# A four-layer graph network on one core: x moved to DRAM during the passes of layers 2 and 3, 12 more row buffers in its place, and their loop issued in program order

## The chip, the core and the metric

The kernel runs on one core of a Trainium2 chip. The metric is device time in microseconds of one execution; the time given is the median of the runs shown. [...]

The engines are called as in the profile: PE is TensorE's matrix multiply and PEld its weight load, DVE is VectorE, ACT is ScalarE, POOL is GpSimd, and SP is SyncE, which here only issues transfers.

## What is computed

6250 nodes with 128 features each pass through four graph layers over the same 200000 edges (src, dst, sorted by dst). Every layer normalises x over its features, applies relu, computes something per edge, sums it per node and adds the result to x. Cut to its core:

```python
h = jnp.maximum(_layernorm(x), 0.0)
x = x + mlp0(h + segment_sum(h[src], dst))                       # layer 0
h = jnp.maximum(_layernorm(x), 0.0)
x = x + mlp1(segment_sum((h @ W_in)[src'] * filter(edge_attr), ...))   # layer 1

h = jnp.maximum(_layernorm(x), 0.0)                              # layer 2
xl, xr = h @ Wl + bl, h @ Wr + br
m = leaky_relu(xl[src] + xr[dst] + edge_weight1 @ We, 0.2)
logits = m @ att
alpha = softmax of logits over the edges of one dst
out = segment_sum(xl[src] * alpha[:, None], dst) + bias_out
x = x + batchnorm(gelu(h + out))

h = jnp.maximum(_layernorm(x), 0.0)                              # layer 3
score = sum(h[dst] * tanh(h[src] + rel[edge_type]), axis=-1)
attn = exp(score - max) / segment_sum(exp(score - max), src)[src]
x = x + leaky_relu((h + segment_sum(attn[:, None] * h[dst], src)) @ W.T, 0.2)
```

## The kernel before

x, the node features, lies in SBUF for the whole kernel as one tile of 128 partitions x 49 x 128 floats (25 KB a partition). Nodes are numbered so that partition p holds nodes 49p to 49p+48.

Each layer first writes the table that its edges read to DRAM (h_tab, y_tab, l_tab and r_tab, g_tab), then runs a pass over the edges. In layers 0, 2 and 3 the pass gathers rows by index; layer 1 computes messages, scatters them to DRAM in the order of src, and reads them back. Layer 3 sums over src and walks the edges in that order, whose indices layer 1 leaves in o_tab and e_tab. The edges are cut into NG = 391 groups of FE = 512 edges, FT = 4 columns of 128 edges each. A group's sums fall on a window of at most 64 neighbouring nodes, so that they are a matrix product with a one-hot matrix, added to an accumulator acc in SBUF at an offset that is loaded as a register. Where the edges aren't sorted as needed, general2 and general3 run in place of windows2 and windows3; with these inputs the window path runs.

Layers 2 and 3 need a softmax over edges. Their passes (sums2, sums3) share the driver in_chunks, which works in chunks of CG = 12 groups and pipelines by steps. In step g it issues, in this order:

- fetch(g): four indirect gathers of 128 rows each into the group's row tile m, issued by POOL (a helper at L298), the load of the window's rows win by SP, every second group the load of a row of indices, and the one-hot matrix hotT on DVE;
- weighted(a) for the oldest group whose softmax weights are known: the one-hot hot on DVE, and in layer 2 the rows scaled by their weights into v on ACT (L1209);
- sums for the group weighted in the step before: PE products ps;
- near(g-1): the PE product pz of hotT and win, four matmuls of two passes each (L1119, L1414), in layer 3 followed by tanh on ACT;
- scores(g-2): on DVE, from pz and m (L1125 to L1128, L1422);
- add: the products of the step before are added into acc on DVE;
- one stage of weights for the chunk whose scores are complete: a generator of six stages in layer 2 (L1136 to L1194), three in layer 3 (L1431 to L1451), one stage a step.

A row tile m is thus in use from its gather until ACT has scaled it (layer 2), or until PE has read it as the stationary operand of ps (L1473, layer 3). The tiles come from a pool mp with 2 x CG + 1 = 25 buffers of 2 KB a partition in layer 2, and 2 x CG + 3 = 27 in layer 3. The other buffers: 4 windows win, 3 pairs of hotT, 3 banks of pz, 2 of ps, 3 of v.

The order in which instructions stand in each engine's queue is chosen by the framework's scheduler, which simulates the program and takes instructions by readiness and priority; the text above gives the priority. Semaphores between engines are placed by the framework too.

After the pass, finish2 and finish3 send the sums of the weights through the small DRAM table d_tab into node order, scale acc, and add the layer's result to x in blocks of CJ = 7 columns. All loads and stores that are not gathers go through the queues of SP and ACT.

Of the kernel before, what the change touches and what calls it, by code (L numbers as in the profile page):

```python
# [9 lines left out]
F32 = mybir.dt.float32  # L10
# [10 lines left out]
D = 128  # L21
# [47 lines left out]
def gnn_kernel(ctx: ExitStack, tc: tile.TileContext, t, out):  # L69
# [74 lines left out]
    def nodes(table):  # L144

        return table[0:NP, :].rearrange("(p j) f -> p j f", j=J)
# [11 lines left out]
    o_tab = dram.tile([IDS - 1, P, NG * FT], I32, name="o_tab")  # L158
    e_tab = dram.tile([2, EP], F32, name="e_tab")
    d_tab = dram.tile([2, NP], F32, name="d_tab")  # L160
    sums = [[dram.tile([ROWS, D], F32, name=f"sum{i}_{k}") for k in range(K)] for i in range(2)]
    softs = [[dram.tile([ROWS, W2], F32, name=f"soft{i}_{k}") for k in range(K)] for i in range(2)]

# [829 lines left out]
    with tc.tile_pool(name="h", bufs=1) as hp, tc.tile_pool(name="y", bufs=2) as yp, \  # L993
            tc.tile_pool(name="y_ps", bufs=2, space=PSUM) as pp:
        h = hp.tile([P, J, D], F32, name="h")
        norm_relu(h)
        nc.scalar.dma_start(nodes(k_tab), h)
        rest = hp.tile([FW, D], F32, name="rest")
        nc.vector.memset(rest, 0.0)
        nc.scalar.dma_start(r_tab[NP:, :], rest)  # L1000
        for c, js in quads:
            if js[0] == c:
                y = yp.tile([P, CJ, D], F32, name="y")
                r = yp.tile([P, CJ, D], F32, name="r")
            u = turned(yp, pp, js, h)
            py = pp.tile([P, 4, 2 * D], F32, name="py")
            for i, j in enumerate(js):
                nc.tensor.matmul(py[:, i, :], ones[0:1, :], b_lr, start=True, stop=False)
                nc.tensor.matmul(py[:, i, :], u[:, i * P:(i + 1) * P], w_lr, start=False, stop=True)
            cs = slice(js[0] - c, js[-1] + 1 - c)  # L1010
            nc.scalar.copy(y[:, cs, :], py[:, :len(js), :D])
            nc.vector.tensor_copy(r[:, cs, :], py[:, :len(js), D:])
            if js[-1] == c + CJ - 1:
                nc.sync.dma_start(nodes(l_tab)[:, c:c + CJ, :], y)
                nc.sync.dma_start(nodes(r_tab)[:, c:c + CJ, :], r)

    def in_chunks(sp, fetch, near, scores, weights, weighted, sums, add):

        sc, ms, todo = None, [], []
        one, two, held = None, None, None
        hot, part = None, None
        g = 0
        while g < NG or one or two or held or todo or hot or part:
            new = (g, fetch(g)) if g < NG else None
            new_hot = None
            if todo:
                a, m, i, ex, scale, more = todo.pop(0)  # L1030
                new_hot = a, weighted(a, m, ex[:, i * FT:(i + 1) * FT], *more), scale
            new_part = (hot[0], sums(hot[0], hot[1]), hot[2]) if hot else None
            new_two = (one[0], near(*one)) if one else None
            if two:
                b, got = two
                i = b % CG
                if i == 0:
                    sc, ms = sp.tile([P, CG * FT], F32, name="sc"), []
                ms.append((b, scores(b, got, sc[:, i * FT:(i + 1) * FT])))
            if part:  # L1040
                add(*part)
            if held:
                try:
                    next(held[0])
                except StopIteration as e:
                    ex, scale, *more = e.value
                    todo += [(a, m, a % CG, ex, scale if i == 0 else None, more)
                             for i, (a, m) in enumerate(held[1])]
                    held = None
            if two and (b % CG == CG - 1 or b == NG - 1):  # L1050
                held = weights(b // CG * CG, len(ms) * FT, sc), ms
                next(held[0])
            one, two, hot, part = new, new_two, new_hot, new_part
            g += 1

    def windows2():

# [7 lines left out]

    def sums2(st, acc):
        lp = st.enter_context(tc.tile_pool(name="ld", bufs=1))
        mp = st.enter_context(tc.tile_pool(name="em", bufs=2 * CG + 1))
        wp = st.enter_context(tc.tile_pool(name="ew", bufs=3))
        rp = st.enter_context(tc.tile_pool(name="er", bufs=2))  # L1070
        sp = st.enter_context(tc.tile_pool(name="es", bufs=2))
# [25 lines left out]
        row = {}  # L1097

        def fetch(g):
            m = mp.tile([P, FT, D], F32, name="m")  # L1100
            for j in range(FT):
                gather(m[:, j, :], l_tab, src[:, g * FT + j:g * FT + j + 1])
            nc.sync.dma_start(win[g % 4][:FW, :], r_tab[bass.ds(starts(g, SP), FW), :])
            h = hots[g // RW % 3]
            if g % RW == 0:
                n = min(RW, NG - g) * FE
                row["d"] = rp.tile([FW, RW * FE], I32, name="row")
                nc.sync.dma_start(row["d"][:, :n], t["dst_row"][:, g * FE:g * FE + n].partition_broadcast(FW))
# [121 lines left out]
    def finish2(acc):  # L1230

        with tc.tile_pool(name="f1", bufs=1) as f1, tc.tile_pool(name="fin", bufs=2) as fp, \
                tc.tile_pool(name="fin_ps", bufs=2, space=PSUM) as pp:
            den = f1.tile([P, J], F32, name="den")
            nc.sync.dma_start(d_tab[0:1, :], acc[0:1, 1, :NP])
            nc.sync.dma_start(den, d_tab[0].rearrange("(p j) -> p j", j=J))
# [388 lines left out]
```

## Time and profile before

| what | us |
|---|---|
| median of 3 runs (9888.56 to 9907.39) | 9891.45 |
| profiled execution, its own time | 11254.5 |
| profiled execution, span from first to last instruction | 11252.7 |
| layer 0, from its first gather to its last | 77.6 to 2432.2 |
| layer 1's read-back products, first to last | 5150.1 to 5828.4 |
| layer 2, gathers, first to last | 6068.1 to 8578.8 |
| layer 2, last product of the sums | 8661.7 |
| layer 3, gathers, first to last | 8789.9 to 11107.3 |
| layer 3, last product of the sums | 11178.5 |

Busy shares of the whole span: PE 74%, PEld 56%, DVE 48%, ACT 18%, POOL 56%.

How to read the views that follow. A line of groups gives source line, engine, operation, tiles and count, then busy us and mean ns of one, then the idle us of the engine just before these instructions and what ended that idle time. "Issue" there means that the profile shows nothing that the engine was waiting for. A line of windows gives a stretch of the span, its length, busy us and count for each engine, the mean granted clock of TensorE (1 is full speed), the busy share of the 16 DMA engines and the GB/s they moved. A line of the timeline gives start, duration, engine, line and operation, with idle time before it in brackets. Some lines can stand for a helper: L298 is the gather of every layer.

### The profile page before, as it was taken

What the parts mean: (1) busy time and instruction counts of PE and PEld (TensorE: products, weight loads), DVE (VectorE), ACT (ScalarE), POOL (GpSimd) and SP (SyncE); (2) the same over time, 40 slices, a digit from 0 to 9 for tenths busy, and PEclk for the clock granted to TensorE, in tenths of its full rate; (3) what the DMA queues carried; (4) which work ended last, traced back from release to release, by engine and by line L of the source; (5) the groups of instructions that cost most, each with busy time, mean ns of one, the idle gap of its engine ahead of it and who ended that gap; (6) DMA issues with size and microseconds to landing.
All of it is one profiled execution on the core that took longest, in us unless ns stands there. A gap on an engine that the chain in (4) does not pass through costs nothing.

```text
span 11252.7 us, 122557 instructions
## 1 busy us (share of the span) xinstructions
PE 8329.9 (74%) x34445; PEld 6310.5 (56%) x34445; DVE 5379.8 (48%) x21948; ACT 1987.7 (18%) x4844; POOL 6250.5 (56%) x6269
## 2 busy tenths in 40 slices
PE   3788888757999988888995666666666267766776
PEld 2444444445666656558982555555555266666665
DVE  4455555413333434334442555555555355555556
ACT  0000000004333434331111122112122111111111
POOL 5666666644666666661003566666663466666663
PEclk9955555555555555555555666666666555555556
DMA  2111111113333333335542222222222233333333
GB/s 66 45 45 44 44 44 44 45 42 92 92 94 93 95 94 94 95 92 139 158 113 67 66 68 69 67 69 68 67 69 60 81 95 95 96 95 94 96 94 88
DMA packets 457374, 893.54 MB, mean 79 GB/s; under 512 B 149642, under 2 KB 231743, under 8 KB 455763
## 3 DMA queue, kind: packets, MB, share of 16 engines
q1 hardware_dynamic: 245552, 456.89, 14.6%
q0 software_dynamic: 200192, 412.80, 13.8%
q10 hardware_dynamic: 10918, 15.65, 0.5%
q8 instruction: 290, 4.75, 0.2%
q14 instruction: 422, 3.46, 0.1%
HBM read 753.95 MB, written 130.80 MB: 79 GB/s over the span
## 4 chain that ended last, share of the span: by engine, by line
PE 55%; issue 13%; DVE 12%; another core or an unknown queue 12%; POOL 3%; DMA 1%; ACT 1%; DVEq 0%; SPq 0%; ACTq 0%; POOLq 0%
PE pw L905 6%; PE ps L959 6%; PE pf L896 6%; PE py L899 6%; PE ps L825 4%; PE ps L1216 4%; PE pz L1119 3%; PE pz L1414 3%; PE ps L1473 3%; POOL m L298 3%; PE pq L778 3%; PE pq L779 2%; PE sizes L746 2%; PE ps L1218 2%
## 5 line engine op out<-in xcount | busy, mean ns | idle before, releaser
L302 POOL DMA_INDIRECT m_tab<-m,pos x1564 | 1569.6, 1004 | 1141.4 <-issue 539.6
L298 POOL DMA_INDIRECT m<-l_tab,src x1564 | 1614.2, 1032 | 1047.9 <-issue 564.7
L298 POOL DMA_INDIRECT m<-g_tab,dst x1564 | 1527.0, 976 | 851.9 <-issue 400.6
L298 POOL DMA_INDIRECT m<-h_tab,src x1564 | 1537.2, 983 | 830.3 <-issue 420.3
L1414 PE MATMUL pz<-win,hotT 128*128 128x128 f32 x3128 | 797.7, 414 | 406.7 <-issue 322.2
L1473 PE MATMUL ps<-hot,m 128*128 128x64 f32 x3128 | 724.0, 402 | 367.5 <-issue 164.3
L825 PEld LDWEIGHTS ps<-hot,m 128*128 128x128 f32 x3128 | 739.3, 327 | 384.8 <-issue 160.0
L899 PEld LDWEIGHTS py<-win,hotT 64*128 64x128 f32 x3128 | 667.8, 313 | 490.5 <-issue 414.7
L1414 PEld LDWEIGHTS pz<-win,hotT 128*128 128x128 f32 x3128 | 678.9, 307 | 449.7 <-issue 436.5
L825 PE MATMUL ps<-hot,m 128*128 128x64 f32 x3128 | 736.8, 411 | 260.5 <-DVE hot L822 101.3
L1473 PEld LDWEIGHTS ps<-hot,m 128*128 128x128 f32 x3128 | 677.9, 315 | 441.3 <-issue 186.8
L1119 PE MATMUL pz<-win,hotT 128*128 128x128 f32 x3128 | 690.8, 373 | 302.3 <-issue 247.6
L905 PEld LDWEIGHTS pw<-L_gnn_W_f,sp_r 128*128 128x128 f32 x3128 | 682.4, 321 | 382.3 <-issue 327.0
L905 PE MATMUL pw<-L_gnn_W_f,sp_r 128*128 128x128 f32 x3128 | 798.5, 434 | 126.7 <-DVE sp_r L931 92.7
L899 PE MATMUL py<-win,hotT 64*128 64x128 f32 x3128 | 775.9, 424 | 135.0 <-issue 107.2
L909 DVE TENSOR_TENSOR m<-pw,L_gnn_b_f_b 128x512 f32<-128x512 f32 x391 | 269.8, 690 | 1226.4 <-PE pw L905 431.6
L1216 PE MATMUL ps<-hot,v 128*128 128x64 f32 x3128 | 604.7, 342 | 273.7 <-issue 198.0
L1209 ACT ACTIVATE v<-m,ex 128x128 f32<-128x128 f32 x1564 | 489.2, 389 | 1762.4 <-remote 873.2
L1119 PEld LDWEIGHTS pz<-win,hotT 128*128 128x128 f32 x3128 | 571.6, 265 | 396.5 <-issue 337.3
L896 PE MATMUL pf<-row_a,L_gnn_W_f 20*128 20x512 f32 x782 | 758.8, 1077 | 23.3 <-DMA row<-in_dst_row 15.3
L1216 PEld LDWEIGHTS ps<-hot,v 128*128 128x128 f32 x3128 | 567.0, 262 | 306.9 <-issue 281.2
L959 PE MATMUL ps<-hot,m 128*128 128x64 f32 x3128 | 671.0, 420 | 18.7 <-DMA m<-m_tab 18.5
(318 smaller groups left out, 12281.2 us busy)
## 6 DMA issues: line engine op xcount, KB each, us to landing
m<-m_tab SPq DMA_DIRECT2D x391, 262.0 KB
row<-in_dst_row SPq DMA_DIRECT2D x390, 256.0 KB
row<-e_tab SPq DMA_DIRECT2D x390, 256.0 KB
row_w<-in_w_row SPq DMA_DIRECT2D x195, 256.0 KB
m<-h_tab,src POOLq DMA_INDIRECT x1564
m_tab<-m,pos POOLq DMA_INDIRECT x1564
m<-l_tab,src POOLq DMA_INDIRECT x1564
m<-g_tab,dst POOLq DMA_INDIRECT x1564
```

The costliest lines, as they stand in the source:

```text
L298: nc.gpsimd.indirect_dma_start(out=dst, out_offset=None, in_=table[:], in_offset=bass.IndirectOffsetOnAxis(ap=idx, axis=0))
L302: nc.gpsimd.indirect_dma_start(out=table[:], out_offset=bass.IndirectOffsetOnAxis(ap=idx, axis=0), in_=src, in_offset=None, **kw)
L825: nc.tensor.matmul(ps, m[:, j, :], hot[:, j, :], start=(j == 0), stop=(j == FT - 1))
L896: nc.tensor.matmul(pf, w_f1, row["a"][:, es], start=True, stop=True)
L899: nc.tensor.matmul(py[:, j, :], hot[:, j * P:(j + 1) * P], w, start=True, stop=True)
L905: nc.tensor.matmul(pw[:, j, :], sp[:, j * P:(j + 1) * P], w_f2, start=True, stop=True)
L959: nc.tensor.matmul(ps, m[:, j, :D], hot[:, j, :], start=(j == 0), stop=(j == FT - 1))
L1119: nc.tensor.matmul(pz[:, j, :], hot[:, j * P:(j + 1) * P], win[g % 4], start=True, stop=True)
L1209: nc.scalar.activation(v[:, j, :], m[:, j, :], AF.Copy, scale=ex[:, j:j + 1])
L1216: nc.tensor.matmul(ps[:, 0, :], v[:, j, :], hot[:, j, :], start=(j == 0), stop=(j == FT - 1))
L1414: nc.tensor.matmul(pz[:, j, :], hot[:, j * P:(j + 1) * P], win[g % 4], start=True, stop=True)
L1473: nc.tensor.matmul(ps[:, 0, :], m[:, j, :], hot[:, j, :], start=(j == 0), stop=(j == FT - 1))
```

## The change

It has five parts.

- A DRAM table x_tab is added. After the normalisation that opens layer 2, x is stored to it through SP's queue; in layer 3 through ACT's queue.
- The pool mp is replaced by a ring of fixed tiles: 25 (27) of its own, followed by 12 that are slices of x, columns 4k to 4k+3 each. Group g uses entry g modulo 37 (39). The last of the 49 columns of x isn't used.
- x_back loads x again from x_tab in seven blocks through SP's queue: in finish2 ahead of everything else, in finish3 after the loads of den.
- The loop of in_chunks is put under manual_schedule for PE, DVE, ACT and POOL: their instructions in the loop keep the order of the text. SP isn't among them.
- The four gathers of a group are issued from the last column to the first.

The general path is not changed. The diff; the loop's body is only indented, which is left out here:

```diff
--- before.py
+++ after.py
@@ -158,6 +158,7 @@
     o_tab = dram.tile([IDS - 1, P, NG * FT], I32, name="o_tab")
     e_tab = dram.tile([2, EP], F32, name="e_tab")
     d_tab = dram.tile([2, NP], F32, name="d_tab")
+    x_tab = dram.tile([NP, D], F32, name="x_tab")
     sums = [[dram.tile([ROWS, D], F32, name=f"sum{i}_{k}") for k in range(K)] for i in range(2)]
     softs = [[dram.tile([ROWS, W2], F32, name=f"soft{i}_{k}") for k in range(K)] for i in range(2)]
 
@@ -995,6 +996,7 @@
         h = hp.tile([P, J, D], F32, name="h")
         norm_relu(h)
         nc.scalar.dma_start(nodes(k_tab), h)
+        nc.sync.dma_start(nodes(x_tab), x)
         rest = hp.tile([FW, D], F32, name="rest")
         nc.vector.memset(rest, 0.0)
         nc.scalar.dma_start(r_tab[NP:, :], rest)
@@ -1014,6 +1016,15 @@
                 nc.sync.dma_start(nodes(l_tab)[:, c:c + CJ, :], y)
                 nc.sync.dma_start(nodes(r_tab)[:, c:c + CJ, :], r)
 
+    def rows_ring(pool, n):
+
+        return [pool.tile([P, FT, D], F32, name=f"m{k}") for k in range(n)] + [
+            x[:, k * FT:(k + 1) * FT, :] for k in range(J // FT)]
+
+    def x_back():
+        for c in range(0, J, CJ):
+            nc.sync.dma_start(x[:, c:c + CJ, :], nodes(x_tab)[:, c:c + CJ, :])
+
     def in_chunks(sp, fetch, near, scores, weights, weighted, sums, add):
 
 
@@ -1023,35 +1034,37 @@
         one, two, held = None, None, None
         hot, part = None, None
         g = 0
-        while g < NG or one or two or held or todo or hot or part:
...
+        order = {mybir.EngineType.PE, DVE, mybir.EngineType.Activation, mybir.EngineType.Pool}
+        with tc.manual_schedule(engines=order):
+            while g < NG or one or two or held or todo or hot or part:
...
 
     def windows2():
 
@@ -1065,7 +1078,7 @@
 
     def sums2(st, acc):
         lp = st.enter_context(tc.tile_pool(name="ld", bufs=1))
-        mp = st.enter_context(tc.tile_pool(name="em", bufs=2 * CG + 1))
+        ring = rows_ring(lp, 2 * CG + 1)
         wp = st.enter_context(tc.tile_pool(name="ew", bufs=3))
         rp = st.enter_context(tc.tile_pool(name="er", bufs=2))
         sp = st.enter_context(tc.tile_pool(name="es", bufs=2))
@@ -1097,8 +1110,8 @@
         row = {}
 
         def fetch(g):
-            m = mp.tile([P, FT, D], F32, name="m")
-            for j in range(FT):
+            m = ring[g % len(ring)]
+            for j in reversed(range(FT)):
                 gather(m[:, j, :], l_tab, src[:, g * FT + j:g * FT + j + 1])
             nc.sync.dma_start(win[g % 4][:FW, :], r_tab[bass.ds(starts(g, SP), FW), :])
             h = hots[g // RW % 3]
@@ -1231,6 +1244,7 @@
 
         with tc.tile_pool(name="f1", bufs=1) as f1, tc.tile_pool(name="fin", bufs=2) as fp, \
                 tc.tile_pool(name="fin_ps", bufs=2, space=PSUM) as pp:
+            x_back()
             den = f1.tile([P, J], F32, name="den")
             nc.sync.dma_start(d_tab[0:1, :], acc[0:1, 1, :NP])
             nc.sync.dma_start(den, d_tab[0].rearrange("(p j) -> p j", j=J))
@@ -1338,6 +1352,7 @@
         h = hp.tile([P, J, D], F32, name="h")
         norm_relu(h)
         nc.sync.dma_start(nodes(g_tab), h)
+        nc.scalar.dma_start(nodes(x_tab), x)
         rest = hp.tile([FW, D], F32, name="rest")
         nc.vector.memset(rest, 0.0)
         nc.scalar.dma_start(g_tab[NP:, :], rest)
@@ -1359,7 +1374,7 @@
 
     def sums3(st, acc, top):
         lp = st.enter_context(tc.tile_pool(name="ld", bufs=1))
-        mp = st.enter_context(tc.tile_pool(name="em", bufs=2 * CG + 3))
+        ring = rows_ring(lp, 2 * CG + 3)
         wp = st.enter_context(tc.tile_pool(name="ew", bufs=3))
         rp = st.enter_context(tc.tile_pool(name="er", bufs=3))
         sp = st.enter_context(tc.tile_pool(name="es", bufs=2))
@@ -1391,8 +1406,8 @@
         row = {}
 
         def fetch(g):
-            m = mp.tile([P, FT, D], F32, name="m")
-            for j in range(FT):
+            m = ring[g % len(ring)]
+            for j in reversed(range(FT)):
                 gather(m[:, j, :], g_tab, dst[:, g * FT + j:g * FT + j + 1])
             nc.sync.dma_start(win[g % 4][:R, :], g_tab[bass.ds(starts(g, SP, first_b), FW), :])
             if g % RW == 0:
@@ -1492,6 +1507,7 @@
             for k in range(2):
                 nc.sync.dma_start(d_tab[k:k + 1, :], acc[k * R:k * R + 1, 1, :NP])
                 nc.sync.dma_start(den[:, k, :], d_tab[k].rearrange("(p j) -> p j", j=J))
+            x_back()
             pt = pp.tile([P, 1], F32, name="pu")
             nc.tensor.matmul(pt, ones[0:1, :], top[:, 0:1], start=True, stop=True)
             last_ = f1.tile([P, 1], F32, name="last_")
```

More of the change, by code (lines that the diff above doesn't have):

```diff
@@ L1025, in in_chunks @@
         g = 0
-        while g < NG or one or two or held or todo or hot or part:
[L1027 to L1043, printed above, removed]
-                    next(held[0])
[L1045 to L1054, printed above, removed]
@@ new lines, in in_chunks @@
+        order = {mybir.EngineType.PE, DVE, mybir.EngineType.Activation, mybir.EngineType.Pool}
+        with tc.manual_schedule(engines=order):
+            while g < NG or one or two or held or todo or hot or part:
+                new = (g, fetch(g)) if g < NG else None
+                new_hot = None
+                if todo:
+                    a, m, i, ex, scale, more = todo.pop(0)
+                    new_hot = a, weighted(a, m, ex[:, i * FT:(i + 1) * FT], *more), scale
+                new_part = (hot[0], sums(hot[0], hot[1]), hot[2]) if hot else None
+                new_two = (one[0], near(*one)) if one else None
+                if two:
+                    b, got = two
+                    i = b % CG
+                    if i == 0:
+                        sc, ms = sp.tile([P, CG * FT], F32, name="sc"), []
+                    ms.append((b, scores(b, got, sc[:, i * FT:(i + 1) * FT])))
+                if part:
+                    add(*part)
+                if held:
+                    try:
+                        next(held[0])
+                    except StopIteration as e:
+                        ex, scale, *more = e.value
+                        todo += [(a, m, a % CG, ex, scale if i == 0 else None, more)
+                                 for i, (a, m) in enumerate(held[1])]
+                        held = None
+                if two and (b % CG == CG - 1 or b == NG - 1):
+                    held = weights(b // CG * CG, len(ms) * FT, sc), ms
+                    next(held[0])
+                one, two, hot, part = new, new_two, new_hot, new_part
+                g += 1
```

## The prediction

> **What bounds the kernel now.** I read four views in this order: busy time by engine, the same for the two loops alone, the groups of the gathers with their idle time, and what the engines waited for. A stretch of the timeline then decides between two readings.
>
> The two loops that the change touches run from 6085 to 8580 us (layer 2) and from 8810 to 11108 us (layer 3), up to their last gathers. The columns are busy us (instructions) of PE, PEld, DVE, ACT and POOL, then the granted clock, the DMA share and GB/s:
>
> ```profile
> 6085.00:8580.00 2495.00, 1564.67 (x9416) 1322.84 (x9417) 1308.12 (x6053) 471.34 (x1530) 1599.12 (x1558) 0.64 0.25 68
> 8810.00:11108.00 2298.00, 1545.25 (x6839) 1419.25 (x6839) 1266.10 (x6237) 237.78 (x473) 1511.23 (x1549) 0.55 0.36 94
> ```
>
> No engine is busy over 68% of either. POOL, which issues the gathers into the row buffers, comes nearest to a limit once its fixed pause is counted:
>
> ```profile
> L298 POOL DMA_INDIRECT m<-l_tab,src x1564 | 1614.2, 1032 | 1047.9 <-issue 564.7
> L298 POOL DMA_INDIRECT m<-g_tab,dst x1564 | 1527.0, 976 | 851.9 <-issue 400.6
> ```
>
> Each gather that waits for nothing still starts 0.30 us after the one before, so 1564 of them cost 469 us of pause. Layer 2: 1614.2 + 469 = 2083 us without any wait, 5.33 us for each of 391 groups. Layer 3: 1527.0 + 469 = 1996 us, 5.11 us a group. The rest is waiting. Layer 2: 1047.9 - 469 - 150 (the wait before the first gather) = 428 us; layer 3: 851.9 - 469 - 61 (the load of dst) = 322 us. These 750 us are what more row buffers aim at. The releasers that the waits name (ACT v L1209, DVE acc L1226, PE ps L1474) are the readers of old rows, or stand just behind them: POOL waits for buffers.
>
> But why do the readers come late? Here are TensorE's waits, layer 2 first (total us, times, longest):
>
> ```profile
> PE ps L1218 <- issue: 273.1, 319, 2.5
> PE pz L1119 <- issue: 247.6, 188, 21.2
> PE ps L1216 <- issue: 198.0, 243, 6.3
> ...
> PE pz L1414 <- issue: 322.2, 272, 20.5
> PE ps L1473 <- issue: 164.3, 127, 4.8
> PE ps L1474 <- issue: 56.8, 76, 1.8
> ```
>
> "Issue" is idle time in which the profile shows nothing to wait for. Layer 2: busy 690.8 + 604.7 + 370.5 = 1666 us, issue idle 719 us, together 2385 us: 93% of the 2577 us from its first matmul to its last addition, and 6.10 us a group against POOL's 5.33. Layer 3: 797.7 + 724.0 + 231.8 = 1753 us and 543 us, together 2297 us: 5.87 us a group against 5.11. In this execution TensorE, with these pauses, is slower than POOL on average, over the whole loop. The pauses look like this, and next to them undisturbed groups:
>
> ```profile
> 7417.34 0.27 PE L1218 MATMUL ps<-hot,ex 128*1 128x64 f32 x1 [0.85 <-issue]
> 7418.76 0.27 PE L1218 MATMUL ps<-hot,ex 128*1 128x64 f32 x1 [1.15 <-issue]
> 7420.17 0.48 PE L1218 MATMUL ps<-hot,ex 128*1 128x64 f32 x3 [1.14 <-issue]
> ...
> 7471.74 2.08 PE L1119 MATMUL pz<-win,hotT 128*128 128x128 f32 x8
> 7473.61 1.81 PE L1216 MATMUL ps<-hot,v 128*128 128x64 f32 x8
> 7475.35 1.01 PE L1218 MATMUL ps<-hot,ex 128*1 128x64 f32 x8
> 7476.29 2.08 PE L1119 MATMUL pz<-win,hotT 128*128 128x128 f32 x8
> ```
>
> Undisturbed, a group takes 7476.29 - 7471.74 = 4.55 us even at the lower clock, less than POOL's 5.33. [...]
>
> [...] The sizes agree: issue idle in both loops is 719 + 543 = 1262 us, and the profiled execution (11254.5 us, span 11252.7) is 1363 us longer than the median, 9891.45. [...]
>
> **The change, part by part.**
>
> *Twelve more row buffers.* A row tile is filled in step g and last read in step g+19 in layer 2 (scores two steps on, the chunk's end up to 11, weights five, one more to the first weighting: ACT v), in g+17 in layer 3 (PE ps). With 25 buffers gather g needs step g-6 done, with 37 step g-18; layer 3 goes from g-10 to g-22. So POOL may run 12 x 5.33 = 64 us further ahead. That absorbs a hiccup of the readers; it doesn't raise their mean rate. Where the readers' mean is the slower (the profile: 6.10 against 5.33), POOL fills the new buffers once and waits as before. Where POOL is the slower (readers 4.55 plus the weights' small matmuls, about 0.2), the old slack of six steps, 32 us, already covers a weights chain (longest pause ended by VectorE there: 12 us). Both ways the loop gains about 0; the gain has a place only between, where the means are equal within some per cent.
>
> *Program order.* The timeline shows pz, ps and the small ps in turn on PE, one group each, and hotT, hot, z, scores, acc on DVE: the order of the text already. POOL has only gathers there. I take 0. The bound above: the weights' matmuls (four places a chunk in layer 2, two in layer 3) stand at a step's end and wait for VectorE's same step, up to 2 us each: 33 x (4 + 2) x 2 = 396 us of PE time, covered while PE's step stays under POOL's. Below: as much gained if today's order had them worse, which the timeline doesn't show.
>
> *Gathers issued last column first.* Same four gathers; the wait for the last reader comes on the first. 0; at most the 43 ns semaphore instructions, which lie inside the pause.
>
> *x to DRAM and back.* x is 128 x 49 x 128 x 4 bytes = 3.21 MB: 10 us at the 322 GB/s of the last row below, 16 us at the 197 of the first.
>
> ```profile
> 5955.00:5976.00 21.00, 20.03 (x42) 9.30 (x40) 3.96 (x7) 2.65 (x6) 0.00 (x0) 0.50 0.47 197
> 8580.00:8662.00 82.00, 77.48 (x500) 67.53 (x498) 42.44 (x208) 31.02 (x100) 0.00 (x0) 0.62 0.06 19
> 8777.00:8787.00 10.00, 0.00 (x0) 0.00 (x0) 0.00 (x0) 1.57 (x2) 0.00 (x0) 0.50 0.90 348
> 11190.00:11200.00 10.00, 0.00 (x0) 0.00 (x0) 0.00 (x0) 0.00 (x0) 0.00 (x0) 0.50 0.82 322
> ```
>
> Store in layer 2, on SP: x is final before the normalisation, SP and the DMA engines are idle until 5955, and the first overwrite comes 25 groups later. 0. Load in layer 2, on SP: slices are last read in step 388 of 411, SP issues nothing from 8587 to 8662, and DMA is at 6% there. 0; if it isn't issued early it stands ahead of the d_tab store and costs 10 us. Store in layer 3, on ACT: x is final at 8741 and ACT is idle to 8757. 0; if it goes beside the g_tab store (90% share), 3.21 MB at 348 GB/s = 9 us before the first gather. Load in layer 3: slices are read up to step 406 of 408, so part of it falls behind the loop, between the loads of den and the broadcast into acc, for which DVE then waits (11190 to 11200). Up to 10 us, I take 5. Work of the finish that today mixes into the tail (seven transposes, 1.7 us, and loads of hs): 3 us more. Sum: +8 us on 9891 (the same on the profiled 11254.5), 9900 rounded. Bounds of this sum: 0 and 10 + 9 + 10 + 4 = 33 us.
>
> **The rivals.**
>
> *A, the forecast: the loops don't move, the borders cost a little.* For it: the means above, and an order that is already the text's. 9900, own range 9880 to 9940.
>
> *B, faster: POOL's waits are real in the timed runs and a good part is covered.* For it: 750 us of waits for buffers stand in the profile, and pauses of 8 to 31 us are shorter than the new 64 us. Against it: on average TensorE is the slower there. All of it would give 9140; a third, 250 us, gives 9640.
>
> *C, slower: program order at the weights' places.* PE waits at a chunk's four (two) places as priced above. It decides from the point where PE's step plus 396 / 782 = 0.5 us passes POOL's: 4.75 + 0.5 = 5.25 against 5.33, so it decides if gathers are quicker without the profiler. A quarter of the 396: 9990.
>
> **How the numbers follow.** A 0.54, B 0.28, C 0.18. The least that a measurement here can tell from no change is about 0.2%, 20 us. A: 0.28 within it, 0.22 slower, 0.04 faster; B: 0.27 faster, 0.01 within; C: 0.17 slower, 0.01 within. Faster 0.31, same 0.30, slower 0.39. The range goes to 9650, which leaves out the better half of B, and to 10000, which leaves out C's worse half.
>
> **What would show it.** In the profile of after: issue idle of TensorE in both loops near 1260 us and POOL's waits still some hundred us (A), or POOL's gathers without waits and the loop shorter by more than 100 us (B), or new PE idle at L1136, L1160, L1171 and L1442 ended by DVE (C). The x loads should lie before 8662 in layer 2 and around the end of the loop in layer 3. If the span of the loops falls by some hundred us with the PE pauses unchanged, my argument on means is wrong.

## The result and the profile after

The changed kernel takes **9950.02 us** (median of 5 runs, 9941.42 to 9968.94) against 9891.45 before: a ratio of 1.0056 with a 95% interval of 1.0045 to 1.0066, so 58.6 us longer. The forecast was 9900, in a range of 9650 to 10000.

One thing has to be said ahead of every comparison. The kernel before took two very different times in these runs, and the difference went with the chip. Beside the changed kernel its executions took 9888 to 9907 us (median 9891), on chip 3 (e9, e10) 9894 to 9909 (9904). On chip 0 (e1 to e4) they took 11221 to 11278 us (11248), on chip 8 (e5 to e8) 11328 to 11394 (11368), on chip 10 (e11, e12) 11337 to 11378 (11361). Below, a chip with one of the first two medians is called an R-chip, since the result has that time, and one with one of the other three an X-chip. The letters stand for these measured times alone: what makes the difference, and whether a chip keeps its time, isn't shown. The profile of before that the prediction read (span 11252.7 us) has the time of an X-chip, the 9891.45 us beside it that of an R-chip. The profile of after has the time of an R-chip. Its fair counterpart is a later profile of the kernel before on an R-chip (run e9_base_look, span 9895.8), and that one is used here. Experiments on X-chips are compared only with the kernel before on the same chip.

Busy time of the engines between the first and the last gather of layer 2 and of layer 3. First the changed kernel, then the kernel before on an R-chip (columns as in the prediction):

```profile
5515.20:7691.00 2175.80, 1570.76 (x9592) 1386.74 (x9592) 1441.22 (x6180) 481.17 (x1565) 1699.45 (x1564) 0.68 0.30 80
7875.00:9854.80 1979.80, 1491.99 (x7015) 1402.96 (x7016) 1360.82 (x6410) 251.96 (x487) 1503.38 (x1564) 0.57 0.42 111
```

```profile
5512.00:7605.00 2093.00, 1511.82 (x9601) 1339.53 (x9602) 1358.76 (x6184) 487.11 (x1565) 1616.63 (x1564) 0.69 0.31 81
7791.80:9785.40 1993.60, 1578.56 (x7016) 1467.02 (x7016) 1345.88 (x6414) 252.15 (x487) 1517.23 (x1564) 0.53 0.42 110
```

The second column is the length. Layer 2 grew by 82.8 us, and POOL's busy time (last bracketed count x1564) by 82.8 us as well; layer 3 shrank by 13.8, POOL by 13.9. So the whole change of both loops is a change in how long the gathers take. (Why those of layer 3 got a little shorter isn't shown.) The rest of the difference between the two spans (9967.1 - 9895.8 = 71.3) is +3.2 before layer 2, -2.8 between the loops and +1.9 behind them; it exceeds the 58.6 us because the profiled execution of the changed kernel was the slowest of its five.

The gathers as groups, changed kernel first, then before on the R-chip. In the changed kernel they are split by the tile that they write, m or x:

```profile
L299 POOL DMA_INDIRECT m<-l_tab,src x1084 | 1180.4, 1089 | 480.4 <-issue 262.4 <-DMA src<-in_src_f 150.4 <-DMA m<-l_tab,src 24.4
...
L299 POOL DMA_INDIRECT m<-g_tab,dst x1084 | 1041.5, 961 | 390.0 <-issue 224.6 <-DMA dst<-o_tab 59.9 <-PE ps L1488 35.7
...
L299 POOL DMA_INDIRECT x<-l_tab,src x480 | 519.1, 1082 | 146.3 <-issue 117.0 <-DMA x<-l_tab,src 9.5 <-ACT v L1222 7.0
```

```profile
L298 POOL DMA_INDIRECT m<-l_tab,src x1564 | 1616.6, 1034 | 627.6 <-issue 516.3 <-ACT v L1209 30.5 <-DVE sc L1128 21.0
...
L298 POOL DMA_INDIRECT m<-g_tab,dst x1564 | 1517.3, 970 | 537.2 <-issue 324.3 <-PE ps L1473 61.0 <-DMA dst<-o_tab 60.9
```

Before, layer 2: idle 627.6 us, of which 151 is the wait before the first gather; the rest, 477, is the pause of 0.30 us 1564 times. **The kernel before has no wait for a buffer in this profile.** The 428 and 322 us that the change was to cover aren't there, and twelve more buffers have nothing to take away. What did change is the mean of one gather in layer 2: 1034 ns before, 1089 and 1082 after, 1087 together.

The pauses of TensorE are not there either. Its waits, changed kernel, then before on the R-chip (us, times, longest):

```profile
PE ps L1229 <- DVE acc L1239: 331.1, 148, 5.6
...
PE pz L1132 <- issue: 29.8, 9, 5.4
```

```profile
PE ps L1216 <- DVE acc L1226: 394.4, 205, 5.9
...
PE pz L1414 <- issue: 54.0, 21, 12.4
...
PE pz L1119 <- issue: 44.8, 14, 5.8
```

TensorE waits for VectorE's additions, which free ps. VectorE in turn waits for rows: in layer 2 of the changed kernel z waits 434.4 us for rows in m and 187.3 us for rows in x. So TensorE has time to spare.

**Where the longer gathers come from.** A stretch of the timeline of the changed kernel, VectorE first, then POOL (start, us, engine, line, operation):

```profile
6487.52 0.33 DVE L1239 TENSOR_TENSOR acc<-acc,ps 128x64 f32 x2
6487.78 0.47 DVE L1124 TENSOR_SCALAR hotT<-row,node 64x512 f32<-64x512 int32 x1
6488.18 0.41 DVE L1219 TENSOR_TENSOR hot<-lane,loc 128x256 f32<-128x256 f32 x1
6491.06 0.69 DVE L1138 TENSOR_TENSOR z<-pz,x 128x512 f32<-128x512 f32 x1 [2.48 <-DMA x<-l_tab,src]
...
6493.36 0.34 DVE L1239 TENSOR_TENSOR acc<-acc,ps 128x64 f32 x2
6493.63 0.47 DVE L1124 TENSOR_SCALAR hotT<-row,node 64x512 f32<-64x512 int32 x1
6494.02 0.41 DVE L1219 TENSOR_TENSOR hot<-lane,loc 128x256 f32<-128x256 f32 x1
```

```profile
6487.75 1.66 POOL L299 DMA_INDIRECT x<-l_tab,src  x1 [0.30 <-DMA x<-l_tab,src]
6489.71 0.94 POOL L299 DMA_INDIRECT x<-l_tab,src  x1 [0.30 <-ACT v L1222]
6490.96 0.94 POOL L299 DMA_INDIRECT x<-l_tab,src  x1 [0.30 <-issue]
6492.21 1.08 POOL L299 DMA_INDIRECT x<-l_tab,src  x1 [0.30 <-DMA x<-l_tab,src]
6493.59 1.66 POOL L299 DMA_INDIRECT x<-l_tab,src  x1 [0.30 <-issue]
```

The two gathers of 1.66 us are those beside which hotT starts 0.03 to 0.04 us later, with hot right behind it. That of 6489.71, beside which these lines show no VectorE instruction, takes 0.94, as does that of 6490.96 beside z. The 0.72 us more are about the length of the pair: from 6487.78 to 6488.59 is 0.81. The same stretch of the kernel before on the R-chip:

```profile
6492.29 0.69 DVE L1125 TENSOR_TENSOR z<-pz,m 128x512 f32<-128x512 f32 x1 [0.84 <-DMA m<-l_tab,src]
6492.89 0.21 DVE L1226 TENSOR_TENSOR acc<-acc,ps 128x64 f32 x1
6493.02 0.69 DVE L1126 SCALAR_TENSOR_TENSOR z<-z 128x512 f32<-128x512 f32 x1
6493.62 0.20 DVE L1226 TENSOR_TENSOR acc<-acc,ps 1x64 f32 x1
6493.75 0.28 DVE L1128 CUSTOM_DVE_ANT_0 z<-z,L_gnn_att_b 128x128 f32<-128x128 f32 x1
```

Here the two additions to acc stand between the instructions on z, and there they cost VectorE no time: two instructions on z start 0.73 us apart with an addition between them (6492.29 to 6493.02), and in the changed kernel 0.73 us apart without one (median). In the written order the additions stand behind the scores, ahead of hotT, and hold hotT up. In the groups without work on the weights in between, it takes 2.315 us from a z to the next hotT before (median of 170 groups) and 2.571 us after (216 groups).

That shift of 0.26 us counts because the loop is tied to the gathers: in 266 of the changed kernel's 391 groups z waits for a gather to land, and a gather of 0.94 us with its pause of 0.30 puts the next one 1.25 us later. Two of them, one held a little, are 2.63 us (6490.96 to 6493.59). So hotT, 2.57 us behind a z that started 0.10 us after a gather, falls into the first hundredths of the next gather but one, and this repeats in many groups. Counted over the loop from the start times in the two traces:

| layer 2, R-chip | most frequent start of hotT against a gather's start | groups there | mean gather there | gathers over 1.45 us | their excess over 0.944 us | excess of the others |
|---|---|---|---|---|---|---|
| before (e9_base_look) | 0.24 us earlier | 128 | 1.08 us | 50 | 40 us | 101 us |
| changed | 0.04 us later | 169 | 1.57 us | 188 | 142 us | 81 us |

142 + 81 - 40 - 101 = 82 us: the growth of the layer 2 loop. The most frequent start moved by 0.28 us, about the 0.26 that the additions account for. No run moved the additions alone, so that it's they and no other difference of the order that shifts hotT is worked out from the traces and not tested. In the changed kernel a hotT that starts 0.09 to 0.22 us after the gather leaves it at 0.94 (27 gathers).

VectorE's own busy time in layer 2 grew by nearly the same amount, from 1358.76 to 1441.22 us, mostly since the additions no longer fit in between. More work on VectorE is not what lengthened the gathers, though: e10 below has 1440.96 us of it and a mean gather of 1.010 us, shorter than in both kernels (1.034 and 1.087).

### The profile page after: what moved, and what is told of

It is laid out like the page before. It is cut to its first block, busy times and chain, and to the rows that moved or that the text cites. A ratio compares the mean times of both kernels' runs of the same rounds, so it can differ in the third digit from the quotient of the medians.

```text
span 9967.1 us, 122332 instructions
## 1 busy us (share of the span) xinstructions
PE 8176.2 (82%) x34445; PEld 6279.3 (63%) x34445; DVE 5521.2 (55%) x21948; ACT 1991.8 (20%) x4844; POOL 6301.6 (63%) x6269
## 4 chain that ended last, share of the span: by engine, by line
DMA 16%; PE 13%; POOL 10%; DVE 9%; issue 6%; ACT 1%; DVEq 0%; POOLq 0%; SPq 0%; ACTq 0%
POOL m L299 7%; PE ps L960 7%; DMA m<-g_tab,dst 6%; DMA m<-l_tab,src 5%; POOL x L299 3%; DMA x<-g_tab,dst 2%; DMA x<-l_tab,src 2%; DVE z L1437 2%; PE ps L1488 1%; DVE z L1138 1%; DVE z L1139 1%; PE ps L1229 1%; DVE z L1141 1%; PE pz L1429 1%; PE py L1010 0%
## 5 line engine op out<-in xcount | busy, mean ns | idle before, releaser
L299 POOL DMA_INDIRECT m<-l_tab,src x1084 | 1180.4, 1089 | 480.4 <-issue 262.4
L299 POOL DMA_INDIRECT m<-g_tab,dst x1084 | 1041.5, 961 | 390.0 <-issue 224.6
L826 PEld LDWEIGHTS ps<-hot,m 128*128 128x128 f32 x3128 | 725.0, 314 | 379.7 <-DMA m<-h_tab,src 186.6
L826 PE MATMUL ps<-hot,m 128*128 128x64 f32 x3128 | 755.1, 403 | 247.4 <-DMA m<-h_tab,src 155.2
L1429 PE MATMUL pz<-win,hotT 128*128 128x128 f32 x3128 | 724.4, 407 | 88.7 <-DVE hotT L1420 71.6
L1132 PE MATMUL pz<-win,hotT 128*128 128x128 f32 x3128 | 681.9, 387 | 55.9 <-issue 29.8
L1488 PE MATMUL ps<-hot,m 128*128 128x64 f32 x2168 | 496.8, 407 | 244.6 <-DVE acc L1497 239.8
L960 PE MATMUL ps<-hot,m 128*128 128x64 f32 x3128 | 671.0, 420 | 19.6 <-DMA m<-m_tab 19.3
L960 PEld LDWEIGHTS ps<-hot,m 128*128 128x128 f32 x3128 | 671.4, 333 | 21.9 <-ACT ids L963 19.6
L1488 PEld LDWEIGHTS ps<-hot,m 128*128 128x128 f32 x2168 | 463.1, 315 | 292.5 <-DVE acc L1497 276.6
```

The costliest lines, as they stand in the source:

```text
L299: nc.gpsimd.indirect_dma_start(out=dst, out_offset=None, in_=table[:], in_offset=bass.IndirectOffsetOnAxis(ap=idx, axis=0))
L826: nc.tensor.matmul(ps, m[:, j, :], hot[:, j, :], start=(j == 0), stop=(j == FT - 1))
L960: nc.tensor.matmul(ps, m[:, j, :D], hot[:, j, :], start=(j == 0), stop=(j == FT - 1))
L1132: nc.tensor.matmul(pz[:, j, :], hot[:, j * P:(j + 1) * P], win[g % 4], start=True, stop=True)
L1429: nc.tensor.matmul(pz[:, j, :], hot[:, j * P:(j + 1) * P], win[g % 4], start=True, stop=True)
L1488: nc.tensor.matmul(ps[:, 0, :], m[:, j, :], hot[:, j, :], start=(j == 0), stop=(j == FT - 1))
```

## The experiments

Runs e1 to e4 were on one X-chip (kernel before: 11247.94 us), e5 to e8 on another (11368.05), e9 and e10 on an R-chip (9903.53), e11 and e12 on an X-chip (11360.93).

**e1_base**: the kernel before, unchanged.

> The kernel before, profiled a second time, to have a profile without TensorE's pauses of unknown cause. If those pauses (1262 us of issue idle in the two loops) belong to the recording, another profile may show few of them: span near 9890 us, POOL's gathers in layers 2 and 3 without waits, pitch 1.33 to 1.36 us in layer 2 and 1.27 us in layer 3. If they belong to the program, the span is again near 11250 us. Theory loop (longer gathers in layer 2 make the 58 us): layer 2's gathers last about 50 us less in sum than the 2176 us after the change. Theory borders: they last the same, and the stretches between the loops are 50 us shorter than after the change.

11235.8 us in the profiled execution; 19 other executions on that chip gave 11221 to 11278. The layer 2 gathers took 2506.5 us with 420 us of waits. Profiled executions of this same kernel thus span 11234.1 us here and 9895.8 us on an R-chip (e9), each as long as the timed executions beside it. So it wasn't the profile that made this kernel slower; the time went with the chip. The gathers themselves last as long as on an R-chip (in layer 2 1.029 and 1.034 us on average).

**e2_order_only, e3_free_order, e4_spill_only**: the change in parts. e2 is the kernel before with the manual schedule; e3 the changed kernel without it; e4 the kernel before with x stored and loaded again, buffers as before.

```diff
 e2 (on before)
+        with tc.manual_schedule(engines=order):
+            while g < NG or one or two or held or todo or hot or part:
 e3 (on after)
-        with tc.manual_schedule(engines=order):
+        if True:
 e4 (on before)
+        nc.sync.dma_start(nodes(x_tab), x)
...
+            x_back()
...
```

> The kernel before with the loop alone put in program order; 25 and 27 pool buffers, x stays. Theory order (the order of DVE and PE in the loop lengthens layer 2's gathers): 9935 to 9960 us, ratio 1.0045 to 1.007. Theory buffers or theory borders: 9885 to 9900 us, ratio within 0.1% of 1.

> The kernel after with the loop's order left to the scheduler again; ring of 37 and 39, x stored and loaded. Theory order: 9890 to 9905 us. Theory buffers (POOL further ahead changes what its gathers meet) and theory borders: 9935 to 9960 us.

> The kernel before with x stored to DRAM and loaded back at the places of the change, though its room isn't used. Theory borders: 9930 to 9960 us. Theory order and theory buffers: 9890 to 9905 us, by my sum up to 33 us more if the loads stand ahead of d_tab.

Measured: order alone 1.0085 [1.0071, 1.0099]; ring and x in DRAM without the order 1.0052 [1.0033, 1.007]; the store and the loads alone 0.9993 [0.9984, 1.0003]. The borders cost nothing that can be seen. The order costs something by itself on this chip: from the first addition to the last, layer 2 takes 2513 us against 2412, and the waits for buffers go from 420 to 514 us. The ring didn't take away the waits (419 us in e3).

**e5_after, e6_hot_late, e7_forward, e8_ring_own**: the changed kernel, and three variants of it. e6 moves the block that makes hot and v behind the scores, so that hot no longer stands right behind hotT; e7 gathers the first column first; e8 keeps the order and the reversed gathers with 25 and 27 buffers of its own; x stays in SBUF and is neither stored nor loaded.

```diff
 e6 (in in_chunks)
-                new_hot = None
-                if todo:
-                    a, m, i, ex, scale, more = todo.pop(0)
-                    new_hot = a, weighted(a, m, ex[:, i * FT:(i + 1) * FT], *more), scale
...
                     ms.append((b, scores(b, got, sc[:, i * FT:(i + 1) * FT])))
+                new_hot = None
+                if todo:
+                    a, m, i, ex, scale, more = todo.pop(0)
+                    new_hot = a, weighted(a, m, ex[:, i * FT:(i + 1) * FT], *more), scale
                 if part:
                     add(*part)
 e7
-            for j in reversed(range(FT)):
+            for j in range(FT):
 e8
-        return [pool.tile([P, FT, D], F32, name=f"m{k}") for k in range(n)] + [
-            x[:, k * FT:(k + 1) * FT, :] for k in range(J // FT)]
+        return [pool.tile([P, FT, D], F32, name=f"m{k}") for k in range(n)]
...
```

> The changed kernel itself once more, on the chip of the other experiments if it is that one (there the kernel before takes 11248 us). If the program order is what costs (the order alone gave 1.0085 [1.0071, 1.0099] there), the ratio is 1.007 to 1.011 and the layer 2 loop's accumulations run about 2510 us from first to last, against 2412 before. If the deeper ring frees GpSimd from its waits once the order is fixed, the ratio is below 1.0 and the waits of 421 and 314 us shrink by more than half. If both add their own loss (order 1.0085 and ring 1.0052), it is about 1.013. On the chip of the result 1.0056 again.

> The changed kernel with the block that makes the one-hot of the second matmul and the scaled rows (hot, v) moved, in the written order, from the start of a step to behind the scores and ahead of the accumulation; nothing else. [...] the gathers over 1.3 us become fewer, the layer 2 mean gather goes from 1.087 us to 1.04 or less, and where GpSimd sets the pace the loop gains 50 to 75 us of 1564 gathers times 0.045. If the position doesn't matter, only the number of VectorE instructions, the mean stays at 1.08 to 1.09 and the time within 10 us of the changed kernel's. On a chip where TensorE sets the pace the mean may change and the time not: then both are within 0.2% of each other.

> The changed kernel with the four gathers of a group in their old order, first column first; nothing else. The prediction put this at nothing: within 10 us of the changed kernel. The rival, that the reversed order lets the ring's first wait (which falls on the last column, read last) come later, or holds the next step's copies up, gives a difference of 30 us or more in the loops of layers 2 and 3, either way.

> Program order, reversed gathers and a ring of the kernel's own 25 and 27 buffers: the node features stay in SBUF, no store and no load of them, no twelve further buffers. If the twelve buffers do nothing (the prediction's forecast), it is within 15 us of the changed kernel. If they take waits of GpSimd away, it is slower than the changed kernel by 50 to 200 us, with waits on row buffers in the loops of 400 to 514 us in layer 2. If the deeper ring costs by itself (GpSimd further ahead, longer end of the loop), it is faster by 20 to 60 us.

| run | ratio to before on that chip | layer 2: mean gather, waits for buffers | first gather to first addition, layers 2 and 3 |
|---|---|---|---|
| e5_after | 1.015 [1.0131, 1.0169] | 1.035 us, 523 us | 245 and 238 us |
| e6_hot_late | 1.0191 [1.0171, 1.0211] | 0.977 us, 669 us | 248 and 240 us |
| e7_forward | 1.0136 [1.0114, 1.0157] | 1.045 us, 502 us | 247 and 238 us |
| e8_ring_own | 1.0093 [1.0074, 1.0111] | 1.042 us, 550 us | 188 and 176 us |

On an X-chip the change costs 1.5%, near the sum of order and ring, 1.4%. The direction of the gathers makes no difference that shows (e5 and e7 overlap). The twelve buffers make it slower: e5 is 63 us above e8, and the store and the loads of x, which e8 lacks too, cost nothing in e4. The table's last column says where: the first addition comes 57 and 62 us later, twelve buffers' worth of gathers (12 x 4 x 1.25 = 60 us). A stretch of e5's timeline from the start of the loop shows why:

```profile
6172.58 0.47 DVE L1124 TENSOR_SCALAR hotT<-row,node 64x512 f32<-64x512 int32 x1
...
6173.15 2.05 PE L1132 MATMUL pz<-win,hotT 128*128 128x128 f32 x8 [17.44 <-issue]
6174.18 0.95 POOL L299 DMA_INDIRECT m<-l_tab,src  x1 [0.30 <-issue]
6175.43 0.94 POOL L299 DMA_INDIRECT m<-l_tab,src  x1 [0.30 <-issue]
...
6190.40 0.94 POOL L299 DMA_INDIRECT m<-l_tab,src  x1 [0.30 <-issue]
6191.65 0.94 POOL L299 DMA_INDIRECT m<-l_tab,src  x1 [0.30 <-issue]
6192.08 0.47 SPq L1116 DMA_DIRECT2D win<-r_tab  x1
6192.08 0.69 DVE L1138 TENSOR_TENSOR z<-pz,m 128x512 f32<-128x512 f32 x1 [19.03 <-remote]
```

The matmuls of one group are recorded with 2.05 us, yet z and the load of win, which both wait for them, start together only 17 us after that record ends, while POOL issues gather after gather. ("Remote" says that the profile names nothing that ended the wait.) This repeats about every 22.5 us for as long as POOL has free buffers. In e8 POOL stops after 25 groups (100 gathers) at 6244.8 us, and the last such pause of TensorE ends at 6254.8; in e5 POOL goes on for 37 groups, and the last pause of this kind ends at 6307.6. Over the same first 184.7 us of the loop, on the R-chip and then on the X-chip, the columns as before:

```profile
5515.20:5699.90 184.70, 98.73 (x520) 87.48 (x521) 121.52 (x455) 23.13 (x73) 144.45 (x133) 0.57 0.31 82
```

```profile
6121.30:6306.00 184.70, 21.94 (x96) 19.76 (x96) 42.28 (x115) 1.28 (x1) 142.02 (x141) 0.52 0.25 62
```

PE is busy for 98.73 and 21.94 us at nearly the same granted clock (0.57, 0.52). On the X-chip TensorE all but stands still in this stretch, in which POOL gathers with next to no break (142.02 us busy and 141 pauses of 0.30), and the deeper ring made the stretch longer.

e6 brought the shorter gathers (0.977 against 1.035 us), but no time: POOL waited the longer for buffers (669 against 523 us). That it is even 58 us slower than e5 isn't explained; the same edit shows it again in e12 below, 63 us above e11.

**e9_base_look, e10_hot_late**: the kernel before and e6's kernel again. These ran on an R-chip.

> The kernel before once more, for a profile. Where it takes about 11250 to 11370 us: as the profile of before, layer 2 loop 2510 us with 420 us of waits for buffers, layer 3 loop 2320. Where it takes about 9890 us (the chip of the result), two theories: if GpSimd's gathers set the pace there for before too and the changed kernel lost by longer gathers of layer 2, the loops of before show no wait for buffers, a mean gather of 1.03 to 1.05 us in layer 2 (changed kernel 1.087) and 0.97 to 0.98 in layer 3 (0.961), that is a layer 2 loop of about 2090 to 2120 us against 2176, and a layer 3 loop of 1990 to 2010 against 1980. If the changed kernel lost elsewhere, the gathers are as long in both, 1.08 to 1.09 us.

> The changed kernel with hot and v behind the scores, once more, for the case that the chip is one where the kernel before takes about 9890 us. There: if hot standing next to hotT lengthens the gathers and the gathers set the pace, the layer 2 mean gather falls from 1.087 to about 0.98 us and the time by up to 1564 times 0.107, some 165 us: ratio 0.985 to 0.995, faster than both kernels. If TensorE then becomes what ends last, the time stays at 1.003 to 1.010. On a chip where the kernel before takes 11250 to 11370 us: 1.019 as in the run before it.

e9: 9897.53 us, no wait for a buffer in either loop, mean gathers 1.034 and 0.970 us, loops 2093.0 and 1993.6 us: the first theory, in every number. e10: **9854.77 us**, ratio **0.9947 [0.9934, 0.9961]**, faster than both kernels. Its loops:

```profile
5506.60:7562.30 2055.70, 1501.41 (x9596) 1324.12 (x9596) 1440.96 (x6183) 481.22 (x1565) 1579.34 (x1564) 0.71 0.32 84
7746.80:9738.70 1991.90, 1504.66 (x7009) 1407.64 (x7010) 1390.29 (x6405) 252.24 (x487) 1515.55 (x1564) 0.56 0.43 110
```

Layer 2 is 120 us shorter than in the changed kernel, all of it POOL's (1699.45 to 1579.34); layer 3, where the place of hot changed too, is 12 us longer. Same instructions, same ring: only the place of hot and v differs. Two groups out of its timeline, VectorE and then POOL:

```profile
6491.92 0.42 DVE L1219 TENSOR_TENSOR hot<-lane,loc 128x256 f32<-128x256 f32 x1
6492.26 0.33 DVE L1239 TENSOR_TENSOR acc<-acc,ps 128x64 f32 x2
...
6492.70 0.46 DVE L1124 TENSOR_SCALAR hotT<-row,node 64x512 f32<-64x512 int32 x1
6493.10 0.67 DVE L1138 TENSOR_TENSOR z<-pz,m 128x512 f32<-128x512 f32 x1
...
6495.38 0.42 DVE L1219 TENSOR_TENSOR hot<-lane,loc 128x256 f32<-128x256 f32 x1
6495.72 0.33 DVE L1239 TENSOR_TENSOR acc<-acc,ps 128x64 f32 x2
6495.98 0.47 DVE L1124 TENSOR_SCALAR hotT<-row,node 64x512 f32<-64x512 int32 x1
```

```profile
6491.56 1.04 POOL L299 DMA_INDIRECT m<-l_tab,src  x1 [0.30 <-issue]
6492.91 1.08 POOL L299 DMA_INDIRECT m<-l_tab,src  x1 [0.30 <-issue]
6494.29 1.02 POOL L299 DMA_INDIRECT m<-l_tab,src  x1 [0.30 <-DMA m<-l_tab,src]
6495.62 1.00 POOL L299 DMA_INDIRECT m<-l_tab,src  x1 [0.31 <-issue]
```

The pair is parted, and hotT falls, in 193 groups, 0.36 us behind a gather's start, as at 6495.98 behind 6495.62, where the mean gather is 1.00 us. Only 4 gathers are over 1.45 us. The edit does two things at once: it parts the pair, and it puts hotT off by the length of hot (2.91 us behind z, against 2.57). How much of the gain comes from each wasn't measured apart. The expectation's 0.98 us and 165 us were too much: 1.010 and 120.

**e11_order_again, e12_order_mixed**: the order alone once more; and the kernel before with the written order, hot late in layer 2 and early in layer 3, buffers and x as before.

```diff
 e12 (on e2)
-                if todo:
+                if todo and not late:
...
+                if todo and late:
+                    a, m, i, ex, scale, more = todo.pop(0)
+                    new_hot = a, weighted(a, m, ex[:, i * FT:(i + 1) * FT], *more), scale
                 if part:
                     add(*part)
...
```

> The program order alone (buffers, gathers and node features as before), once more, for the case that the chip is one where the kernel before takes about 9900 us. If the order is the whole loss, the ratio is 1.005 to 1.008 as with the changed kernel (1.0056), with a layer 2 mean gather of 1.08 to 1.09 us and no wait for a buffer in the loops. If the order costs only together with the ring or the reversed gathers, it is 0.998 to 1.001 with a mean of 1.03 to 1.05. On a chip where the kernel before takes 11250 to 11370 us: 1.0085 again.

> The kernel before with the loop in written order, hot and v of layer 2 behind the scores and ahead of the accumulation, those of layer 3 at the start of a step as in the change; buffers, gathers and node features as before. Where the kernel before takes about 9900 us: layer 2 mean gather 1.01 us as in the run with both moved (1.010), layer 3 mean 0.961 as in the changed kernel (before 0.970), so 2093 to about 2056 and 1994 to about 1980: 45 to 55 us under before, ratio 0.9945 to 0.996 if the twelve further buffers do nothing; about 1.0 if those buffers were what gained in the run with both moved. On a chip where the kernel before takes 11250 to 11370 us: 1.010 to 1.015.

Both ran on an X-chip: 1.0074 [1.006, 1.0088] and 1.0142 [1.012, 1.0165], as expected for that case. The traces from X-chips still answer one question. With the order alone, 113 gathers of layer 2 are over 1.45 us (e11; 108 in e2), with hotT starting within 0.1 us of 110 of the 113. The kernel before has 31 and 25 of them on X-chips, the ring without the order 25 (e3), and the order with hot late, without the ring, 3 (e12). So the hold-up follows from the order and the place of hot, not from the ring. What the order alone costs on an R-chip, and whether e12 would beat e10 there, wasn't measured.

## Why the prediction was right or wrong

**The time** lies in the range, 50 us above the forecast, but by luck: the one cost in the sum, 8 us for the borders, came to nothing, and the 58.6 us come from loops that were put at 0 (+82.8 us in layer 2, -13.8 in layer 3, in the profiled executions). The likeliest case, A, isn't what happened. Rival C (slower, through program order, 9990) has the right cause in the wrong place: not TensorE at the weights' matmuls but VectorE's additions, hotT and hot.

**What bounds the kernel: wrong for the timed runs.** The reading that TensorE with its pauses is slower than POOL (6.10 against 5.33 us a group) holds for an X-chip. The step that failed is to read 1262 us of pauses and 1363 us of excess, since they are of a size, as one thing that the timed runs don't have. On an R-chip and on an X-chip a profiled execution takes as long as the timed ones (9897.53 beside 9894 to 9909; 11235.8 beside 11221 to 11278), so the 1363 us are no cost of the profile but the difference between R-chip and X-chip times. The agreement of the two sums persuaded, but one of them was itself only an unexplained difference. (The undisturbed group of 4.55 us, "at the lower clock", ran at a granted clock of 0.50 in the profile of before; from 7401.74 to 7409.14 us the clock was 1.00 and three groups took 2.47 us each.)

**Twelve more buffers, 0: right on the R-chip**, by the branch that the prediction gave second: where POOL is the slower, there is no wait to cover. (The pauses of 8 to 31 us named under B are no waits of POOL's: apart from one of 40.5 and one of 34.1 us, those lasted 7.5 us at most in the profile of before.) POOL's 2083 and 1996 us without a wait were what the R-chip's loops took, 2093 and 1994. On the X-chip of e5 and e8 the first branch has a cost that it missed: POOL filled the new buffers once, and the readers, held up meanwhile, began 57 and 62 us later.

**Program order, 0: wrong, the step that decided.** "The order of the text already" holds for PE, but for VectorE it misreads the profile. The trace of before shows the additions to acc between the instructions on z in 623 of 728 cases (for instance one at 7473.02, between instructions on z at 7472.42 and 7473.15); the text puts them behind the scores. Moving them made no instruction of a group longer by more than 9 ns on average, but put hotT off by 0.26 us behind z: 82 us in layer 2. The bound that was given (up to 396 us) priced another place. The waits at the weights' places are there (82.3 us at L1149, 46.1 at L1173, 68.2 at L1448) but TensorE has that time to spare.

**The means of 1032 and 976 ns as constants: wrong.** The sums of 2083 and 1996 us keep the length of a gather from before; it came out at 1087 and 961. In the trace hotT and hot together lengthen a gather by 0.72 us (0.94 to 1.66), and which instructions stand next to each other, and when, is just what a new order changes.

**Gathers last column first, 0: right** as far as measured (e5 and e7 don't differ on an X-chip). **Store and loads, +8 of 0 to 33: right**, with 0 the better value (e4). In the changed kernel the layer 2 loads are issued from 7614.2 to 7665.2 us, inside the loop. In layer 3 they go from 9867.7 to 9889.9, between the last gather (9854.8) and the last addition (9892.8): the 5 us taken for that place weren't spent, since matmuls and additions ran on beside them.

**What would show it.** The prediction named POOL gathers without waits as the mark of rival B. They came, without B's gain: on an R-chip they were without waits before (e9).

## What to carry to other kernels

Before a wait in a profile is priced, compare the profile's time with the timed runs; where they differ by a seventh, as here (11254.5 and 9891.45 us), the two may have run under different conditions, and a profile of the same kernel as long as the timed runs (here e9) is worth more than any theory of the gap. The mean duration of the instructions that set the pace isn't a constant: that of the same gathers was 1034, 1087 and 1010 ns under three orders (e9, the changed kernel, e10). So look at which instructions of other engines start beside them, and ask what a reordering does to that phase. Once such an order is written out by hand, moving one block can be worth more than the buffers: here a ratio of 1.0056 became 0.9947 with the same work on R-chips, while on an X-chip the same move went from 1.015 to 1.0191.

## What the hardware showed that was not expected

- The same program takes 9891 to 9904 us (medians) on R-chips and 11248 to 11368 on X-chips, with gathers that last as long one by one (1.034 and 1.029 us in layer 2, e9 and e1). Layer 0, which the change doesn't touch, shows it alone: from the start of its first gather to that of its last are 2010 us in the profile of after (R-chip) and 2355 in that of before (X-chip). Why isn't known.
- In e5 and e8, on an X-chip, with POOL gathering without a wait, the four pz matmuls of a group release their readers 17 to 20 us after hotT, and a group takes about 22.5 us, as long as 18 gathers; with POOL waiting, z's of successive groups come 2.7 to 4.6 us apart (ten of them in e8). Why isn't known.
- In the changed kernel on an R-chip a gather was held by hotT and hot together for 0.72 us where hotT started 0.03 to 0.04 us after it, as in the stretch above (over the 169 groups about that start the mean gather is 1.57 us), and it took 0.94 us, as without them, where hotT started 0.09 to 0.22 us after it (27 gathers). With hotT alone in the first place (e10, 11 groups) it took 1.25 us on average, so it seems that hot, coming directly behind, prolonged the hold. Gathers were held beside other VectorE instructions too: in nine groups of the changed kernel with hotT about 0.25 us behind the gather's start, scans of the weights (L1180, L1181) run from 0.13 us before that start to 0.32 us behind it, and the gather takes 1.85 us; in four groups with the same start of hotT and no scans it takes 0.94.
